# A graph network's last layer: the weight product moved from before the edge sum to behind it

## The chip, the cores and the metric

The kernel runs on one core of a Trainium2 chip. A core has a matrix engine (TensorE, PE in the profile, with its weight loads as PEld), a vector engine (VectorE, DVE), a scalar engine (ScalarE, ACT), GpSimd (POOL), which here issues the indirect loads, and SyncE (SP), which issues the plain ones; sixteen DMA engines move the data. The metric is device time of one execution in microseconds (us), less is better. Times in the profile count from the start of its span.

## The reference

A graph of N = 4096 nodes with D = 512 features and E = 65536 edges, sorted by destination, goes through four layers, each with a layer norm and a ReLU ahead of it and a residual sum behind it. Layers 0 (attention), 1 and 2 (messages) are not changed. The last layer is:

```python
# ahead of it: h = maximum(layernorm(x), 0)
row = concatenate([src, arange(n)]); col = concatenate([dst, arange(n)])   # each node is its own neighbour too
deg = segment_sum(ones, row, n)
dis = rsqrt(deg)
norm = dis[row] * dis[col]
z   = h @ W.T + b                                    # 512 x 512
out = segment_sum(norm[:, None] * z[row], col, n)
x   = x + relu(out)
```

The factor dis[col] is the same for all edges of one destination and can stand outside the sum. So can the product with W, since it is linear: the sum of dis[row] * (h[row] @ W.T + b) is (the sum of dis[row] * h[row]) @ W.T plus (the sum of dis[row]) * b.

## The kernel before, in words

All is float32. The 4096 nodes are 32 blocks of 128 rows, the 65536 edges 512 tiles of 128, and four tiles are a group (U = 4, 128 groups). A float32 array `acc` holds 32 x 530 numbers per partition in SBUF: one row of sums per node, of which the first 512 columns are used by the layers here. Under `manual_schedule` each engine runs its instructions in the order in which the code issues them, and SP's queue is ordered likewise.

**Layer 2's end** (`layer2_ends`, from 4578 to 5104 us of the profile) works through 16 pairs of blocks as a software pipeline: pass p of its loop does the first step of pair p, the second of pair p-1, and so on.

- Pair p: `load_h` (L1203) loads two blocks of h into `h_sb` (three buffers; `h2_sb` in the code). `turned` (L1251) transposes them on PE, 8 transposes of 128x128 into PSUM tile `tr`, and ACT copies them to `h_t` (L1253). The same for two blocks of `acc` (`a_t`). POOL then adds b4 to `h_sb` in place.
- Pair p-1: PE multiplies both by w3 into `u_ps` (L1276), ACT puts it into `zu` with the bias and computes the activation.
- Pair p-2: PE multiplies by w4 into `o_ps` (L408, `product`), DVE adds the two blocks of `h_sb` to it (L1294) and with that frees the buffer. A norm, the residual, the store of x3 (L1308), and the norm of layer 3 follow on DVE; the normed rows stay in `h3`.
- Pair p-4, layer 3's beginning: `turned` transposes `h3` with a ReLU on the way out, PE multiplies by layer 3's weights `wl_sb` into `o_ps` (L408), ACT multiplies by dis into `acc` (L1322), DVE adds dis * b (L1323), and SP stores the pair to the DRAM table `ztab` (L1324), rows of 512 floats.

**Layer 3's edge loop** (`sum_edges`, 5104 to 5869 us). For each tile POOL issues one indirect DMA (L419) that gathers 128 rows of `ztab`, by the edges' sources, into `g` (six buffers of four tiles), four groups ahead. One group ahead, ACT makes the one-hot matrices of the edges' places in their window of 128 destinations (L863 four times, L864 once per group; `oh`, three buffers). PE multiplies each one-hot with its gathered rows (L887), adding up a group of four tiles in one PSUM bank `sum_ps` (four banks). A group's window spans at most two blocks, so `add_window` adds the bank twice to `acc`, each with a mask of rows and the block's number read from a register (L431, on DVE). `acc` begins with the node's own row, from layer 2's end.

Inside this loop, after every second tile, `follow` is called. `Ending` closes a block b once the tiles are past a fixed place, `END_AT + END_STEP * b` = 230 + 10 b: ACT computes relu(dis * acc) into `t_end` (L1352), DVE adds x3's block, loaded ahead by SP into `x_end` (L1339), and SP stores it to the output (L1359). That these places are late enough for the data is checked on the device by `too_late`; data for which they are not would go through a general path behind it, which the inputs here do not take.

The same `sum_edges` serves layer 1 (1204 to 1996 us). There a class `Between` does the next layer's begin inside the loop, block by block: transposes, a copy by ACT to `ht_mid` (L980) and two products into `pq_ps` (L985).

Of the kernel before, what the change touches and what calls it, by code (L numbers as in the profile page):

```python
# [10 lines left out]
F32 = mybir.dt.float32  # L11
BF16 = mybir.dt.bfloat16
# [22 lines left out]
def kernel(  # L35
# [34 lines left out]
    PAIR = 2  # L70
    NW = NG // PAIR

    END_AT, END_STEP = 230, 10
    assert N == 4096 and E == 65536 and D == 512 and W == 512
    DA = D + H + 2
    HW = DA // 2
# [182 lines left out]
    def by_destination(pool, ppool):  # L259

        ends = pool.tile([P, 2, W], I32, name="ends_d")
        for j, of in enumerate((src, dst)):
            nc.sync.dma_start(ends[:, j, :], of.rearrange("(p c) -> p c", p=P))
        yield
        three = pool.tile([P, 3, W], F32, name="three_d")
        for j in range(2):
            nc.vector.tensor_copy(three[:, j, :], ends[:, j, :])
            yield
        loc_i = pool.tile([P, W], I32, name="loc_i")
        nc.vector.tensor_scalar(loc_i, ends[:, 1, :], P - 1, None, op0=OP.bitwise_and)  # L270
# [35 lines left out]
        for r in range(2):  # L306
            at = -(-(END_AT + END_STEP * r) // U)
            rows.append((first[:1, at::2 * END_STEP // U], P * (r + 1), 2 * P))
        too_late(pool, wide, rows)
        nc.vector.tensor_copy(odd[:, 1:2], wide)  # L310
        yield
# [542 lines left out]
    nc.vector.tensor_scalar(s_loc, s_loc, -1.0, None, op0=OP.mult)  # L854


    def sum_edges(table, idx, loc, bi, half, per, beside=None, follow=None):

        def made_one_hots(pool, minus, t0):

            oh = pool.tile([P, U, P], F32, name="oh")
            for j in range(U):
                nc.scalar.activation(oh[:, j, :], row_i, AF.Abs, bias=minus[:, t0 + j:t0 + j + 1])  # L863
            nc.scalar.activation(oh, oh, AF.Relu, scale=-1.0, bias=1.0)  # L864
            return oh

        with tc.tile_pool(name="edge", bufs=3) as ep, tc.tile_pool(name="edge_ps", bufs=4, space=PSUM) as eps, \
                tc.tile_pool(name="beside", bufs=1) as bp, \
# [3 lines left out]
            side = Side(*(beside(bp, bps) if beside else ()))  # L872
            for i in range(-4, NG):
                if i + 4 < NG:
                    g = got[i + 4] = ep.tile([P, U, D], F32, name="g", bufs=6)
                    for j in range(U):
                        t = (i + 4) * U + j
                        gather(g[:, j, :], table, idx[:, t:t + 1])
                if 0 <= i + 1 < NG:
                    ohs[i + 1] = made_one_hots(ep, loc, (i + 1) * U)  # L880
                if i < 0:
                    continue
                g, oh = got.pop(i), ohs.pop(i)
                if i % per == 0:
                    ps = eps.tile([P, D], F32, name="sum_ps")
                for j in range(U):
                    nc.tensor.matmul(ps, oh[:, j, :], g[:, j, :], start=i % per == 0 and j == 0,  # L887
                                     stop=i % per == per - 1 and j == U - 1)
# [299 lines left out]

        messages(begun)

    ztab = dram.tile([N, D], F32, name="ztab")
    x3 = dram.tile([N, D], F32, name="x3")
    def layer2_ends():
        with ExitStack() as end:
# [62 lines left out]
            end.enter_context(tc.manual_schedule(engines=ENGINES))  # L1257
            groups = NB // R
            h_t, a_t, u, xs, h3 = {}, {}, {}, {}, {}
            for p in range(groups + 4):  # L1260
                now = lambda k: 0 <= k < groups
                if now(p):
                    if p not in h:
# [33 lines left out]
                if now(p - 2):  # L1297
# [13 lines left out]
                    h3[p - 2] = lp.tile([P, R, D], F32, name="h3", bufs=3)  # L1311
                    for j in range(R):
                        norm.rows(j, h3[p - 2][:, j, :], xt[:, j, :])
                if now(p - 4):
                    b0 = (p - 4) * R
                    h3_t = turned("h3_t", h3.pop(p - 4), AF.Relu)
                    for j in range(R):
                        o_ps = lps.tile([P, D], F32, name="o_ps")
                        product(o_ps, h3_t[:, :, j * P:(j + 1) * P], wl_sb)
                        y = acc[:, b0 + j, :D]  # L1320
                        d = dis[:, b0 + j:b0 + j + 1]
                        nc.scalar.activation(y, o_ps, AF.Copy, scale=d)  # L1322
                        nc.vector.scalar_tensor_tensor(y, bl_bc, d, y, op0=OP.mult, op1=OP.add)  # L1323
                    nc.sync.dma_start(blocks_of(ztab, b0, R), acc[:, b0:b0 + R, :D])  # L1324

    layer2_ends()

    class Ending:


        def __init__(self, pool, ahead):
            self.pool, self.ahead, self.next, self.xs, self.ready = pool, ahead, 0, {}, []
# [16 lines left out]
        def begin(self):  # L1349
            b, self.next = self.next, self.next + 1  # L1350
            t = self.pool.tile([P, D], F32, name="t_end", bufs=4)
            nc.scalar.activation(t, acc[:, b, :D], AF.Relu, scale=dis[:, b:b + 1])  # L1352
            self.ready.append((b, t))

        def finish(self):
            for b, t in self.ready:
                xt = self.xs.pop(b)
                nc.vector.tensor_add(xt, xt, t)
                nc.sync.dma_start(out[b * P:(b + 1) * P, :], xt)  # L1359
                self.load(b + self.ahead)  # L1360
            self.ready = []

        def the_rest(self):
            self.finish()
            while self.next < NB:
                self.begin()
                self.finish()

    nc.vector.tensor_scalar(d_loc, d_loc, -1.0, None, op0=OP.mult)
    with tc.tile_pool(name="l3_end", bufs=1) as lp:  # L1370
        ending = Ending(lp, 6)
        sum_edges(ztab, d_src, d_loc, d_bi, d_half, 1, follow=ending.follow)
        ending.the_rest()

    @with_exitstack
    def in_general(ctx):
# [23 lines left out]
        def sums(table, k_from, k_to):  # L1400
            with tc.tile_pool(name="sums", bufs=1) as pool, tc.tile_pool(name="sums_ps", bufs=1, space=PSUM) as ppool:
                with tc.For_i(0, W, 1) as t:
                    rows = pool.tile([P, D], F32, name="rows_g")
                    gather(rows, table, number_of(pool, k_from, t))
                    over_blocks(pool, ppool, k_to, t, rows, 1)

        nc.sync.dma_start(by, stab.rearrange("k p w -> p k w"))
        for j in range(2):
# [111 lines left out]
                over_blocks(pool, ppool, 1, t, m, 1)  # L1520

        layer2_ends()
        sums(ztab, 0, 1)
        with tc.tile_pool(name="l3_late", bufs=1) as lp:
            Ending(lp, 6).the_rest()

    other = const.tile([1, 1], F32, name="other")
    nc.vector.reduce_max(other, odd, axis=AX.X)
# [39 lines left out]
```

## Time and profile before

| | us |
|---|---|
| median of nine runs | 5847.4 |
| lowest and highest of them | 5838.24, 5867.2 |
| the profiled execution | 5870.75 |
| its span in the profile | 5868.9 |
| PE, DVE, ACT, POOL busy | 5173.5, 3529.3, 3372.3, 2903.2 |
| layer 3's edge loop: matmuls L887, busy | 516.1 |
| its gathers L419, busy | 486.6 |

The profiled execution is one run, 23 us above the median, so differences are worked out in it and then put on the median. A row of the profile's groups reads: line, engine, operation, the tile written and the tiles read, how often; then busy time, mean ns of one, and the idle time of the engine just before them with what ended most of it. In a timeline a row begins with its start and its length, and the bracket at its end is the idle time before it and what released it. An f32 matmul of the program appears as two records, each a pass with its own weight load. "remote" and "issue" stand where the profile names no other engine.

### The profile page before, as it was taken

How to read it: one execution, taken by the hardware profiler on the slowest of the kernel's cores; microseconds unless marked ns; L12 is line 12 of the kernel's file. 1: busy time of each engine (PE TensorE's matmuls, PEld its weight loads, DVE VectorE, ACT ScalarE, POOL GpSimd, SP SyncE). 2: the span in 40 equal slices, each digit the busy share in tenths (PEclk: the TensorE clock that was granted, in tenths of full speed). 3: DMA queues.
4: the chain of work that ended last, by engine and by line, in shares of the span. 5: the costliest groups of instructions: out<-in, count | busy, mean ns of one | idle time of the engine just before them, and what ended most of it. 6: DMA issues, size and time to landing. Idle time of an engine off the chain costs nothing.

```text
span 5868.9 us, 56747 instructions
## 1 busy us (share of the span) xinstructions
PE 5173.5 (88%) x17274; PEld 2844.0 (48%) x17274; DVE 3529.3 (60%) x5843; ACT 3372.3 (57%) x5157; POOL 2903.2 (49%) x2604
## 2 busy tenths in 40 slices
PE   7678888869989799999999999999999899866676
PEld 4456666634434355555555555555555666422222
DVE  8566666623233377777777777777777456422223
ACT  1245555524334378888888888888888433333333
POOL 0255555456666465555555555555553111266665
PEclk9789899989999899999999999999999999988888
DMA  3356565467777565555555555555553212266676
GB/s 108 107 171 180 173 184 176 146 189 234 230 232 233 160 134 116 113 116 113 116 113 115 115 114 115 113 115 113 115 113 69 86 65 72 95 183 181 208 223 185
DMA packets 345928, 842.24 MB, mean 144 GB/s; under 512 B 61072, under 2 KB 77456, under 8 KB 345616
## 3 DMA queue, kind: packets, MB, share of 16 engines
q0 software_dynamic: 237568, 673.35, 47.0%
q1 hardware_dynamic: 108048, 165.19, 8.2%
q8 instruction: 140, 2.29, 0.2%
q14 instruction: 172, 1.41, 0.1%
HBM read 753.14 MB, written 85.20 MB: 143 GB/s over the span
## 4 chain that ended last, share of the span: by engine, by line
PE 68%; another core or an unknown queue 6%; ACT 3%; issue 3%; DVE 2%; DMA 1%; DVEq 1%; POOL 0%; SPq 0%; ACTq 0%; POOLq 0%
PE m_ps L408 30%; PE sum_ps L887 10%; PE small_ps L1084 4%; PE small_ps L1111 4%; PE o_ps L408 4%; PE tr_ps L1091 4%; PE u_ps L1276 4%; PE pq_ps L985 3%; PE sum_ps L696 2%; ACT oh L863 1%; DVE acc L431 1%; PE tr_ps L1074 1%; PE tr L1251 1%; ACT oh L864 1%
## 5 line engine op out<-in xcount | busy, mean ns | idle before, releaser
L408 PE MATMUL m_ps<-w_sb,h_t 128*128 128x512 f32 x4096 | 1820.8, 592 | 0.5 <-ACT h_t L1093 0.5
L887 PE MATMUL sum_ps<-g,oh 128*128 128x512 f32 x2048 | 1010.6, 636 | 257.6 <-ACT oh L864 103.2
L408 PEld LDWEIGHTS m_ps<-w_sb,h_t 128*128 128x128 f32 x4096 | 757.6, 190 | 809.3 <-issue 797.6
L419 POOL DMA_INDIRECT pg<-ptab,d_src x512 | 498.3, 973 | 993.5 <-ACT h_t L1093 817.0
L1067 POOL DMA_INDIRECT pg<-qtab,d_dst x512 | 871.4, 1702 | 158.2 <-issue 154.4
L419 POOL DMA_INDIRECT rows<-htab,s_dst x512 | 484.1, 945 | 654.4 <-issue 368.2
L887 PEld LDWEIGHTS sum_ps<-g,oh 128*128 128x128 f32 x2048 | 412.5, 205 | 802.2 <-issue 577.6
L696 PE MATMUL sum_ps<-rows,oh 128*128 128x261 f32 x2048 | 555.4, 423 | 198.2 <-DVE rows L690 123.8
L419 POOL DMA_INDIRECT g<-ytab,s_dst x512 | 485.3, 948 | 333.3 <-issue 132.8
L419 POOL DMA_INDIRECT g<-ztab,d_src x512 | 486.6, 950 | 329.6 <-issue 137.7
L696 PEld LDWEIGHTS sum_ps<-rows,oh 128*128 128x128 f32 x2048 | 412.1, 209 | 298.5 <-DVE rows L690 134.0
L1093 ACT COPY h_t<-tr_ps 128x512 f32<-128x512 f32 x512 | 275.2, 589 | 429.3 <-PE tr_ps L1091 429.2
L431 DVE SCALAR_TENSOR_TENSOR acc<-sum_ps,d_half,acc 128x512 f32 x256 | 192.3, 751 | 546.7 <-remote 275.5
L431 DVE SCALAR_TENSOR_TENSOR acc<-sum_ps,s_half,acc 128x522 f32 (+1 forms) x256 | 193.3, 755 | 406.5 <-PE sum_ps L887 257.6
L1143 DVE TENSOR_TENSOR pg<-pg,small_ps 128x512 f32<-128x512 f32 x512 | 318.3, 682 | 189.7 <-PE small_ps L1084 153.1
L1111 PE MATMUL small_ps<-parts,oh 128*128 128x512 f32 x1024 | 311.1, 446 | 13.4 <-DVE oh L414 13.4
L985 PE MATMUL pq_ps<-w_sb,ht_mid 128*128 128x512 f32 x512 | 270.5, 615 | 58.7 <-ACT ht_mid L980 54.4
L1105 DVE TENSOR_TENSOR parts<-z,parts 128x1024 fp32r<-128x1024 f32 x256 | 313.6, 1225 | 8.9
L863 ACT ACTIVATE oh<-row_i,d_loc 128x128 f32<-128x128 f32 x512 | 162.3, 387 | 269.7 <-remote 182.2
L1091 PEld LDWEIGHTS tr_ps<-ident,pg 128*128 128x128 f32 x2048 | 240.2, 141 | 146.2 <-issue 146.2
L1180 DVE TENSOR_TENSOR pg<-pg,qg 128x1024 f32<-128x1024 f32 x256 | 301.3, 1218 | 0.7 <-ACT qg L1177 0.7
L431 DVE SCALAR_TENSOR_TENSOR acc<-small_ps,d_half,acc 128x512 f32 x256 | 192.4, 751 | 161.4 <-issue 135.2
(281 smaller groups left out, 7959.3 us busy)
## 6 DMA issues: line engine op xcount, KB each, us to landing
eg<-in_edge_attr_dram SPq DMA_DIRECT2D x128, 128.0 KB
xt<-in_x_dram SPq DMA_DIRECT2D x8, 1024.0 KB
htab<-acc SPq DMA_DIRECT2D x32, 256.0 KB
x_row<-in_x_dram SPq DMA_DIRECT2D x32, 256.0 KB
rows<-htab,s_dst POOLq DMA_INDIRECT x512
x<-x_row SPq DMA_DIRECT2D x32, 256.0 KB
ytab<-acc SPq DMA_DIRECT2D x32, 256.0 KB
x_mid<-x SPq DMA_DIRECT2D x32, 256.0 KB
```

What stands on the lines that cost most here:

```text
L408: nc.tensor.matmul(ps, h_t[:, k, :], w_sb[:, k0 + k, :], start=start and k == 0, stop=stop and k == KC - 1)
L419: nc.gpsimd.indirect_dma_start(out=dst_ap, out_offset=None, in_=table, in_offset=bass.IndirectOffsetOnAxis(ap=idx, axis=0))
L431: nc.vector.scalar_tensor_tensor(at, ps, half[:, k, i:i + 1], at, op0=OP.mult, op1=OP.add)
L696: nc.tensor.matmul(ps[:, c, :HW], oh[:, j + k, :], rows[:, j + k, c * HW:(c + 1) * HW], start=j + k == 0, stop=j + k == GT - 1)
L887: nc.tensor.matmul(ps, oh[:, j, :], g[:, j, :], start=i % per == 0 and j == 0, stop=i % per == per - 1 and j == U - 1)
L985: nc.tensor.matmul(ps, h_t[:, k, :], self.w1_sb[:, k0 + k, :], start=k == 0, stop=k == KC - 1)
L1067: nc.gpsimd.indirect_dma_start(out=pg[:, j, :], out_offset=None, in_=qtab, in_offset=bass.IndirectOffsetOnAxis(ap=d_dst[:, t:t + 1], axis= ...
L1091: nc.tensor.transpose(h_ps[:, k, :], h[:, j, k * P:(k + 1) * P], ident)
L1105: nc.vector.tensor_sub(parts[:, 1], m, parts[:, 0].bitcast(F32))
L1111: nc.tensor.matmul(ps, oh[:, j, :], parts[j // 2][:, k, j % 2, :], start=j == 0 and k == 0, stop=j == U - 1 and k == 1)
L1143: nc.vector.tensor_add(nxt[:, j], nxt[:, j], ps)
L1180: nc.vector.tensor_mul(h[i][:, half], h[i][:, half], qg[:, half])
```

## The change

The transposes of `h3`, the product with `wl_sb` and its bias are taken out of layer 2's end. There ACT now writes relu(h3) * dis straight to `acc`, one pass of the pipeline earlier (pair p-3), and SP stores it to `ztab`. The table's rows get two more floats, which hold three bf16 numbers (and a fourth, not used) whose sum is dis, written once ahead of the pairs; column D of `acc` begins with dis, and the next two with zero.

In the edge loop a gather brings 514 floats. ACT makes a second one-hot in bf16 (`oh_short`), PE multiplies it with the three bf16 numbers into `tail_ps` ahead of the group's main matmuls, and DVE adds that to three more columns of `acc`, by `add_window` as for the rows.

`Ending` gets seven steps, one per call of `follow`: four transposes of acc's block into `turn_end`; ACT's copy to `ht_end`; two steps of two matmuls with `wl_sb` into `o_end`; the sum of the three columns times b, added to it, on DVE; ReLU and dis on ACT; the residual and the store. Its places are 150 + 20 b for the first eight blocks and 230 + 10 b as before for the others. `turn_end` and `o_end` have one PSUM bank each, the loads of x3 run four blocks ahead instead of six, and `wl_sb` and `bl_bc` are loaded at the start of `Ending`. The places' check and the general path are changed accordingly.

```diff
-    END_AT, END_STEP = 230, 10
+    ENDS = (0, 150, 20, 8), (8, 230, 10, NB)
+    def end_of(b):
+        return next(at + step * b for first, at, step, last in ENDS if b < last)
...
+    def tail_at(b):
+        return acc[:, ds(b, 1), D:D + 3].rearrange("p b d -> p (b d)")
...
             for j in range(U):
                 nc.scalar.activation(oh[:, j, :], row_i, AF.Abs, bias=minus[:, t0 + j:t0 + j + 1])
+            short = None
+            if tail:
+                short = pool.tile([P, U, P], BF16, name="oh_short")
+                nc.scalar.activation(short, oh, AF.Relu, scale=-1.0, bias=1.0)
             nc.scalar.activation(oh, oh, AF.Relu, scale=-1.0, bias=1.0)
...
-                    g = got[i + 4] = ep.tile([P, U, D], F32, name="g", bufs=6)
+                    g = got[i + 4] = ep.tile([P, U, D + tail], F32, name="g", bufs=6)
...
+                if tail:
+                    tail_ps = bps.tile([P, 3], F32, name="tail_ps", bufs=2)
+                    for j in range(U):
+                        nc.tensor.matmul(tail_ps, short[:, j, :], g[:, j, D:].bitcast(BF16)[:, :3],
+                                         start=j == 0, stop=j == U - 1)
                 for j in range(U):
-                    nc.tensor.matmul(ps, oh[:, j, :], g[:, j, :], start=i % per == 0 and j == 0,
+                    nc.tensor.matmul(ps, oh[:, j, :], g[:, j, :D], start=i % per == 0 and j == 0,
                                      stop=i % per == per - 1 and j == U - 1)
                     if j == U - 1 and i % per == per - 1:
+                        if tail:
+                            add_window(i, bi, half, tail_at, tail_ps)
                         add_window(i // per, bi, half, row_at, ps)
...
-    ztab = dram.tile([N, D], F32, name="ztab")
+    ztab = dram.tile([N, D + 2], F32, name="ztab")
...
-            wl_sb = load_w(wp, "wl_sb", w_l3t)
-            bl_bc = row_bc(wp, "bl_bc", b_l3)
+            three = wp.tile([P, NB, 4], BF16, name="dis_parts")
+            rest = wp.tile([P, NB], F32, name="dis_rest")
+            nc.vector.tensor_copy(rest, dis)
+            for k in range(3):
+                nc.vector.tensor_copy(three[:, :, k], rest)
+                nc.vector.tensor_sub(rest, rest, three[:, :, k])
+            nc.vector.tensor_copy(three[:, :, 3], rest)
+            nc.sync.dma_start(ztab[:, D:].rearrange("(b p) c -> p b c", p=P), three.bitcast(F32))
+            nc.vector.tensor_copy(acc[:, :, D], dis)
+            nc.vector.memset(acc[:, :, D + 1:D + 3], 0.0)
...
-            for p in range(groups + 4):
+            for p in range(groups + 3):
...
-                if now(p - 4):
-                    b0 = (p - 4) * R
-                    h3_t = turned("h3_t", h3.pop(p - 4), AF.Relu)
+                if now(p - 3):
+                    b0 = (p - 3) * R
+                    hh = h3.pop(p - 3)
                     for j in range(R):
-                        o_ps = lps.tile([P, D], F32, name="o_ps")
-                        product(o_ps, h3_t[:, :, j * P:(j + 1) * P], wl_sb)
-                        y = acc[:, b0 + j, :D]
-                        d = dis[:, b0 + j:b0 + j + 1]
-                        nc.scalar.activation(y, o_ps, AF.Copy, scale=d)
-                        nc.vector.scalar_tensor_tensor(y, bl_bc, d, y, op0=OP.mult, op1=OP.add)
-                    nc.sync.dma_start(blocks_of(ztab, b0, R), acc[:, b0:b0 + R, :D])
+                        nc.scalar.activation(acc[:, b0 + j, :D], hh[:, j, :], AF.Relu,
+                                             scale=dis[:, b0 + j:b0 + j + 1])
+                    nc.sync.dma_start(ztab[b0 * P:(b0 + R) * P, :D].rearrange("(b p) d -> p b d", p=P),
+                                      acc[:, b0:b0 + R, :D])
...
+        def block(self, b):
+            pool = self.pool
+            ps = self.ppool.tile([P, KC, P], F32, name="turn_end", bufs=1)
+            for k in range(KC):
+                nc.tensor.transpose(ps[:, k, :], acc[:, b, k * P:(k + 1) * P], ident)
+            yield
+            h_t = pool.tile([P, KC, P], F32, name="ht_end", bufs=2)
+            nc.scalar.copy(h_t, ps)
+            yield
+            ps = self.ppool.tile([P, D], F32, name="o_end", bufs=1)
+            for k in range(KC):
+                nc.tensor.matmul(ps, h_t[:, k, :], self.wl_sb[:, k, :], start=k == 0, stop=k == KC - 1)
+                if k % 2:
+                    yield
+            s = pool.tile([P, 1], F32, name="s_end", bufs=2)
+            nc.vector.reduce_sum(s, acc[:, b, D:D + 3], axis=AX.X)
+            t = pool.tile([P, D], F32, name="t_end", bufs=2)
+            nc.vector.scalar_tensor_tensor(t, self.bl_bc, s, ps, op0=OP.mult, op1=OP.add)
+            yield
+            nc.scalar.activation(t, t, AF.Relu, scale=dis[:, b:b + 1])
+            yield
+            xt = self.xs.pop(b)
+            nc.vector.tensor_add(xt, xt, t)
+            nc.sync.dma_start(out[b * P:(b + 1) * P, :], xt)
+            self.load(b + self.ahead)
...
         def follow(self, tiles):
 
-            if tiles % 4:
-                return
-            self.finish()
-            while self.next < NB and tiles >= END_AT + END_STEP * self.next:
-                self.begin()
+            if self.next < NB and not tiles % U and tiles >= end_of(self.next):
+                self.going.append(self.block(self.next))
+                self.next += 1
+            self.step()
```

More of the change, by code (lines that the diff above doesn't have):

```diff
@@ L305, in by_destination @@
         rows = []
-        for r in range(2):
-            at = -(-(END_AT + END_STEP * r) // U)
-            rows.append((first[:1, at::2 * END_STEP // U], P * (r + 1), 2 * P))
+        for b0, _, step, b1 in ENDS:
+            by = 1 if step % U == 0 else 2
+            for r in range(by):
+                at = -(-end_of(b0 + r) // U)
+                last = min(NG, at + (b1 - b0 - r - 1) // by * (by * step // U) + 1)
+                rows.append((first[:1, at:last:by * step // U], P * (b0 + r + 1), by * P))
         too_late(pool, wide, rows)
@@ L854, with sum_edges @@
     nc.vector.tensor_scalar(s_loc, s_loc, -1.0, None, op0=OP.mult)
-    def sum_edges(table, idx, loc, bi, half, per, beside=None, follow=None):
+    def sum_edges(table, idx, loc, bi, half, per, beside=None, follow=None, tail=0):
         def made_one_hots(pool, minus, t0):
@@ L1339, in load @@
                 nc.sync.dma_start(self.xs[b], x3[b * P:(b + 1) * P, :])
-        def follow(self, tiles):
-            if tiles % 4:
-                return
-            self.finish()
-            while self.next < NB and tiles >= END_AT + END_STEP * self.next:
-                self.begin()
[L1349 to L1361, printed above, removed]
-        def the_rest(self):
[L1364 to L1367, printed above, removed]
+        def block(self, b):
[23 more added lines that the diff above has]
+            self.load(b + self.ahead)
@@ new lines, in step @@
+        def step(self):
+            for w in list(self.going):
+                if next(w, StopIteration) is StopIteration:
+                    self.going.remove(w)
+        def follow(self, tiles):
+            if self.next < NB and not tiles % U and tiles >= end_of(self.next):
+                self.going.append(self.block(self.next))
+                self.next += 1
+            self.step()
+        def the_rest(self):
+            while self.next < NB or self.going:
+                if self.next < NB:
+                    self.going.append(self.block(self.next))
+                    self.next += 1
+                self.step()
+                self.step()
@@ L1369 @@
     nc.vector.tensor_scalar(d_loc, d_loc, -1.0, None, op0=OP.mult)
-    with tc.tile_pool(name="l3_end", bufs=1) as lp:
-        ending = Ending(lp, 6)
-        sum_edges(ztab, d_src, d_loc, d_bi, d_half, 1, follow=ending.follow)
+    with tc.tile_pool(name="l3_end", bufs=1) as lp, tc.tile_pool(name="l3_end_ps", bufs=1, space=PSUM) as lps, \
+            tc.manual_schedule(engines=ENGINES):
+        ending = Ending(lp, lps, 4)
+        sum_edges(ztab, d_src, d_loc, d_bi, d_half, 1, follow=ending.follow, tail=2)
@@ L1398, in over_blocks, with sums @@
                     nc.vector.tensor_add(at, at, ps)
-        def sums(table, k_from, k_to):
+        def sums(table, k_from, k_to, tail=0):
             with tc.tile_pool(name="sums", bufs=1) as pool, tc.tile_pool(name="sums_ps", bufs=1, space=PSUM) as ppool:
                 with tc.For_i(0, W, 1) as t:
-                    rows = pool.tile([P, D], F32, name="rows_g")
+                    rows = pool.tile([P, D + tail], F32, name="rows_g")
                     gather(rows, table, number_of(pool, k_from, t))
-                    over_blocks(pool, ppool, k_to, t, rows, 1)
+                    if tail:
+                        wide = pool.tile([P, DA], F32, name="wide_g")
+                        nc.vector.memset(wide[:, D:], 0.0)
+                        nc.vector.tensor_copy(wide[:, :D], rows[:, :D])
+                        nc.vector.tensor_copy(wide[:, D:D + 3], rows[:, D:].bitcast(BF16)[:, :3])
+                        over_blocks(pool, ppool, k_to, t, wide, 2)
+                    else:
+                        over_blocks(pool, ppool, k_to, t, rows, 1)
         nc.sync.dma_start(by, stab.rearrange("k p w -> p k w"))
@@ L1522, in in_general @@
         layer2_ends()
-        sums(ztab, 0, 1)
-        with tc.tile_pool(name="l3_late", bufs=1) as lp:
-            Ending(lp, 6).the_rest()
+        sums(ztab, 0, 1, 2)
+        with tc.tile_pool(name="l3_late", bufs=1) as lp, tc.tile_pool(name="l3_late_ps", bufs=1, space=PSUM) as lps:
+            Ending(lp, lps, 4).the_rest()
     other = const.tile([1, 1], F32, name="other")
```

10 lines of the change are left out of this document (6 added, 4 removed).

## The prediction

> **What bounds the kernel now.** First the page, by slices and groups: which engine fills which part of the span. Then the busy times of three stretches, for the clock and for which engine leads. Then the timeline at the two places that the change touches.
>
> ```profile
> PE   7678888869989799999999999999999899866676
> POOL 0255555456666465555555555555553111266665
> PEclk9789899989999899999999999999999999988888
> ...
> L419 POOL DMA_INDIRECT g<-ztab,d_src x512 | 486.6, 950 | 329.6 <-issue 137.7
> ...
> L985 PE MATMUL pq_ps<-w_sb,ht_mid 128*128 128x512 f32 x512 | 270.5, 615 | 58.7 <-ACT ht_mid L980 54.4
> ```
>
> The last five slices (146.7 us each) are layer 3's edge loop: PE 6 to 7 tenths, POOL as much, a lower clock. The slices before them (layer 2's end) have PE at 8 to 9 and hardly any POOL.
>
> ```profile
> core 0: us, PE busy (x) PEld busy (x) DVE busy (x) ACT busy (x) POOL busy (x), PEclk, DMA share, GB/s
> 4800.00:4900.00 100.00, 96.66 (x377) 65.28 (x376) 56.75 (x136) 40.10 (x47) 13.99 (x6) 1.00 0.19 64
> 5200.00:5300.00 100.00, 66.38 (x140) 28.27 (x139) 26.20 (x35) 32.75 (x88) 66.33 (x71) 0.86 0.64 185
> 5700.00:5800.00 100.00, 72.94 (x150) 30.25 (x149) 29.72 (x41) 37.74 (x97) 67.70 (x72) 0.87 0.74 223
> ```
>
> So layer 2's end (4578 to 5104 us) is bound by PE at full clock, and the loop (5104 to 5869) is not. A gather takes 0.95 us and the next follows 0.30 later: 512 x 1.25 = 640 us of the loop's 765. The change takes PE work out of the first stage and puts it into the second. Its worth is what the first can give up less what the second can't hide.
>
> **Layer 2's end: what goes.** A steady pair of blocks takes 31.55 us. The removed part (8 transposes 0.87, the wait for ACT's copy 1.11, 16 passes of 0.43) is 9.02 us by the timeline, 4871.11 to 4880.13. But that work covers a load. h_sb (h2_sb in the code) has three buffers, so the load for pair p+1 is issued only after DVE's second add (L1294) of pair p-2, which is right behind the w4 product; then the removed products run. Where there are none yet (pairs 3 and 4) the profile shows what is left:
>
> ```profile
> 4624.04 0.69 DVE L1294 TENSOR_TENSOR acc<-h_sb,o_ps 128x512 f32<-128x512 f32 x1 [2.69 <-PE o_ps L408]
> 4624.81 0.36 SPq L1203 DMA_DIRECT2D h_sb<-h  x1
> 4628.73 1.94 PE L1251 MATMUL tr<-ident,h_sb 128*128 128x128 f32 x8 [4.72 <-DMA h_sb<-h]
> ...
> 4654.44 0.36 SPq L1203 DMA_DIRECT2D h_sb<-h  x1
> ...
> 4657.97 1.94 PE L1251 MATMUL tr<-ident,h_sb 128*128 128x128 f32 x8 [4.28 <-DMA h_sb<-h]
> ```
>
> PE waits 4.72 and 4.28 us for h_sb, then runs at half clock (eight transposes 1.94 instead of 1.04) for 3.4 to 6.8 us. From 4628.73 to 4657.97 is 29.24 us per pair. I take 31.55 - 9.02 + 4.5 + 1.6 (half clock) = 28.6; ends 22.5 (load hidden) and 29.24. Pair 15 is then turned at 4657.97 + 11 x 28.6 = 4972.6, 24.1 us of its iteration follow, and the last u product (13.82) ends at 5010.5, where before has 5051.8: 41 earlier. Behind it before needs 52.3 us to its last ztab store (two more rounds of products); after needs the w4 product 6.9, DVE's chains of the last two pairs (14.7 and 13.6) and two Relus of about 0.7: 36.5. Together -41 - 16, taken as **-56** (with all pairs at 29.24: -50; with the load hidden: -115). The bf16 parts of dis are ten small DVE operations and one 4096-row store ahead of pair 0; the nearest row, the store of 4096 x 32 B at L560, was 2.6 us of packets. The wl loads go from the same place: nothing, -3 to +3.
>
> **Layer 3's loop, tiles up to 310.** Added per group: one ACT Relu (0.63 as L864), four bf16 passes (eight of L656 took 0.42: 0.21), two DVE adds with a register address (0.82 apart as L431's), and eight blocks in all. PE, DVE and ACT are idle for a third to two thirds of this stretch, so the pace of 1.44 us per tile hides them, except that the Relu stands in ACT's restart, once per 20 tiles: 15 x 0.63 = **+9**. Rows of 2056 instead of 2048 B: htab's 2080 B gathers took 0.94 us of all 16 DMA engines against 0.905, and DMA is busy 0.64 to 0.74, so hidden; without that cover 512 x 0.03 = 15. Bounds -45 (pace 1.29, near the 1.25 of POOL, if the denser PE ends the pauses shown next) to +20 (blocks prolong eight pauses).
>
> ```profile
> 5822.94 10.57 PE L887 MATMUL sum_ps<-g,oh 128*128 128x512 f32 x24 [0.81 <-ACT oh L864]
> ...
> 5830.54 0.95 POOL L419 DMA_INDIRECT g<-ztab,d_src  x1 [0.30 <-issue]
> ...
> 5834.82 3.28 DVE L431 SCALAR_TENSOR_TENSOR acc<-sum_ps,d_half,acc 128x512 f32 x4 [10.41 <-PE sum_ps L887]
> 5835.06 0.94 POOL L419 DMA_INDIRECT g<-ztab,d_src  x1 [3.58 <-remote]
> ...
> 5840.74 2.08 PE L887 MATMUL sum_ps<-g,oh 128*128 128x512 f32 x2 [7.24 <-issue]
> ```
>
> This is the loop's cycle, every 28.6 us: PE does three groups in a row (24 passes), yet DVE and POOL see the first of them done only when PE has stopped and 1.3 us have gone. PE's completions come late, POOL runs out of g buffers for 3.6 us, and 20 gathers take 25 + 3.6.
>
> **Tiles 310 to 512: a block every 10 tiles.** A pass of 128x512 takes 0.43 and an f32 product two of them (1024 records for 512 tiles). PE's own work per block is 10 x 0.857 + 2.5 x 0.21 (tails) + 4 x 0.108 (transposes) + 8 x 0.43 (product) = 12.96 us, under the 14.4 that ten tiles take now. But the transposes stand in PE's queue right behind a group's last matmul and read acc, which DVE's row adds of that same group write at register addresses: PE must wait for DVE, which waits for PE. Queued behind them are all later matmuls, and so g buffers and gathers. The price: two adds 1.57 and some 0.4 of handover, 1.95, if the completion comes at once (5858.09, after the last matmul, does); about 1.6 more with the late completions above: 3.55. Then the product waits for ACT's copy of the turned block; layer 1's loop has that wait (L985) at 54.4 us in 32 blocks, 1.7 each. Here half a group of matmuls lies more between: I take half, 0.85. Sum 17.4 per block, 20.2 x 17.4 = 351 us against 291 now: **+60**. Ends: the pace stays 14.4 (0), and 22 (+153), where DVE has the adds of two or three groups (3.3 each with the tails) to catch up on before the transposes may run.
>
> **Drain and start.** Before ends its last add 5 us after the last matmul. After: block 28's turning and blocks 29 to 31 come behind it, one turn_end and one o_end bank, so about 5.0 each (0.43 + 0.59 + 3.43 and handovers), then STT, Relu, add (0.75, 0.72, 0.68) and waits: 26.5, **+22** (ends +14, +30). Start: 1.25 MB of wl and bl stand on SP ahead of x_end and share the DMA with the first gathers: **+3** (0 to 8).
>
> **Sum:** -56 + 9 + 60 + 22 + 3 = +38 us. The profiled execution took 5870.75 (span 5868.9) and would take 5909; the median of the nine runs is 5847.4, so 5885.
>
> A rule that speaks against this sum: the Trainium skill, "TensorE: Matmul & The Clock Gate", section "Why this matters for your kernels", says that PE idle for more than about 3 us falls back to half clock. The trace agrees on its sides: 4.28 us of idle was followed by half clock, the waits of 2.0 to 2.85 us in layer 1's loop left the clock at 0.98. By the rule each block's 3.55 us would also cost 1.7 to 3.4 us, an estimate of +34 to +69 on top; my sum takes none, since 3.55 lies between those two rows.
>
> **Rivals.** (1) *The loop hides the blocks*, faster: PE has 1.44 us of room per block under the gathers' 14.4, and if the late completions end because POOL then pauses at other times, the turning costs no more than that. It decides at a wait of 1.45 us per block. Then -56 + 9 + 0 + 22 + 3 = -22, 5825; with a better early pace down to 5790. For it: the last groups' completions were prompt. Against: two adds alone are 1.57. (2) *Near tie*: all waits of a block cost 2.5 us, what layer 1's loop shows (16 tiles 23.5 us, PE work 21.0): 15.5 per block, +22 instead of +60, so 5847. (3) *The load is hidden after all*: -115 instead of -56, 5826. Against: both uncovered pairs waited. (4) *DVE catches up*: 20 to 22 per block, +113 to +153, so 5938 to 5978. For it: the quoted cycle, with two groups' adds in one go and PE idle 7.24 us.
>
> **Chances.** Forecast 0.42, (1) 0.22, (2) 0.11, (3) 0.07, (4) 0.18. Faster by over 0.2% (11.7 us, about what can be told from no change): (1) and (3), 0.29; within: (2) and a little of the forecast's low end, 0.13; slower: 0.58. The range cuts the ends of (1) and the upper half of (4): 5800 to 5950; the forecast's own is 5860 to 5915.
>
> **What would show it.** The steps in the changed profile: PE waiting 4 to 5 us for h_sb in every pair, pairs 28 to 29 us apart; the first gather at 5050 instead of 5108; tiles 310 to 512 in 335 to 370 us, with turn_end's transposes waiting for DVE's acc and o_end's matmuls for ht_end; 20 to 30 us from the last sum matmul to the end. Pairs of 23 us, or blocks at 14.4 us, would make it wrong towards faster; PE idle of over 7 us before each block's transposes towards slower.

## The result and the profile after

The changed kernel takes 5944.42 us (median of ten runs) against 5849.5 for the kernel before: a ratio of 1.0158, interval 1.0141 to 1.0175. It is 1.6% slower where 0.64% slower was forecast; 95 us stand against a sum of 38. The profiled execution has a span of 5964.4 us. Its slices:

```profile
PE   7678788869999799999999999999999888576788
...
POOL 0255555356666465555555555555551111665553
PEclk9789989989999899999999999999999889788899
```

Layer 2's end (slices 32 to 34) now has a clock of 8 to 9 tenths where it had 9; over the stage the mean is 0.89 instead of 0.99. The loop's share of POOL falls from 6 tenths to 5 behind its first third.

Later runs fell on chips of two kinds, which this comparison didn't show: on one kind the kernel before takes 5789 to 5865 us, on the other 5420 to 5424. The result above is of the first, slow kind. Each chip was used in one session only, so whether the chip itself makes the kind is not shown; "slow" and "quick" stand for what was measured there. Stages are compared within a kind. All stages are read from the traces, one execution for each column, in us:

| | slow: before | after | quick: before | after |
|---|---|---|---|---|
| layer 2's end, first transposes to first gather | 526.1 | 491.5 | 526.4 | 494.7 |
| first gather to first sum matmul | 7.2 | 10.2 | 7.4 | 10.4 |
| tiles 0 to 150 | 219.9 | 233.9 | 183.7 | 183.8 |
| tiles 150 to 310 | 231.6 | 273.6 | 201.1 | 211.3 |
| tiles 310 to 512 | 290.3 | 331.8 | 254.1 | 324.8 |
| last sum matmul to the end | 11.4 | 33.0 | 12.4 | 32.9 |
| span | 5868.9 | 5964.4 | 5421.9 | 5493.5 |

On the slow chip the stages give +87.5; the other 8 us lie ahead of layer 2's end, in code that is the same. On slow chips a stage with gathers differs by a few us from run to run: tiles 0 to 150 take 231 to 239 us in the traces of the changed kernel and of the experiments that leave these tiles alone.

The timeline of the changed kernel at the head of a steady pair in layer 2's end:

```profile
4813.51 0.36 SPq L1222 DMA_DIRECT2D h_sb<-h  x1
...
4817.97 1.94 PE L1278 MATMUL tr<-ident,h_sb 128*128 128x128 f32 x8 [5.21 <-DMA h_sb<-h]
...
4819.70 1.91 PE L1278 MATMUL tr<-ident,acc 128*128 128x128 f32 x8
...
4821.41 3.12 PE L1303 MATMUL u_ps<-h_t,w_sb 128*128 128x256 f32 x8
...
4824.37 1.89 PE L1303 MATMUL u_ps<-a_t,w_sb 128*128 128x256 f32 x8
```

PE waits 5.21 us for the load, and from 4817.97 to about 4823.8 it runs at half clock: both sets of transposes take 1.9 instead of 1.04, the first eight passes 3.12 instead of 1.89. The pair takes 30.7 us.

The same kernel in the loop, where a block comes every 20 tiles:

```profile
5359.65 3.68 PE L904 MATMUL sum_ps<-g,oh 128*128 128x512 f32 x8
...
5365.56 0.75 DVE L436 SCALAR_TENSOR_TENSOR acc<-sum_ps,d_half,acc 128x512 f32 x1 [2.80 <-issue]
...
5369.81 0.22 DVE L436 SCALAR_TENSOR_TENSOR acc<-tail_ps,d_half,acc 128x3 f32 x1 [3.50 <-issue]
5370.09 0.94 POOL L424 DMA_INDIRECT g<-ztab,d_src  x1 [2.59 <-remote]
...
5371.61 1.57 DVE L436 SCALAR_TENSOR_TENSOR acc<-sum_ps,d_half,acc 128x512 f32 x2 [0.67 <-DVE acc L436]
...
5373.32 1.09 PE L1371 MATMUL turn_end<-ident,acc 128*128 128x128 f32 x4 [9.99 <-DVE acc L436]
...
5374.35 4.91 PE L904 MATMUL sum_ps<-g,oh 128*128 128x512 f32 x8
```

The group's matmuls end at 5363.3, DVE adds them at 5371.61, and only then can PE turn the block: 9.99 us idle, and half clock after it (8 passes 4.91 instead of 3.68). DVE is not adding all this time: it is busy for 2.7 of the 9.99 us, and ahead of the two operations marked "issue" it sat idle for 2.80 and 3.50 us without waiting for anything that the profile shows. In the nine waits of 9.87 to 10.42 us, one for each block from tile 150 to 312, DVE is busy 2.0 to 3.5 us.

Ahead of the first sum matmul:

```profile
5088.84 0.16 PE L901 MATMUL tail_ps<-g,oh_short 128*128 128x3 bf16 x1 [31.36 <-DMA g<-ztab,d_src]
...
5092.10 0.16 PE L901 MATMUL tail_ps<-g,oh_short 128*128 128x3 bf16 x1 [0.97 <-DMA g<-ztab,d_src]
```

The four tail matmuls of a group stand ahead of its sum matmuls, so the first sum matmul now waits for the fourth gather, 3.3 us after the first. And behind the last sum matmul:

```profile
5934.62 0.63 PE L1371 MATMUL turn_end<-ident,acc 128*128 128x128 f32 x4 [2.63 <-DVE acc L436]
...
5942.65 1.96 PE L1378 MATMUL o_end<-wl_sb,ht_end 128*128 128x512 f32 x4 [0.93 <-DVE s_end L1382]
...
5947.70 1.95 PE L1378 MATMUL o_end<-wl_sb,ht_end 128*128 128x512 f32 x4 [0.93 <-DVE t_end L1384]
...
5952.74 3.67 PE L1378 MATMUL o_end<-wl_sb,ht_end 128*128 128x512 f32 x8 [0.93 <-DVE t_end L1384]
...
5958.05 0.69 DVE L1389 TENSOR_TENSOR x_end<-x_end,t_end 128x512 f32<-128x512 f32 x1 [0.85 <-ACT t_end L1386]
```

The products start 5.05 us apart, each waiting for the one o_end bank.

### The profile page after: what moved, and what is told of

Same layout as the page of the kernel before. It is cut to its first block, busy times and chain, and to the rows that moved or that the text cites. A ratio compares the mean times of both kernels' runs of the same rounds, so it can differ in the third digit from the quotient of the medians.

```text
span 5964.4 us, 59542 instructions
## 1 busy us (share of the span) xinstructions
PE 5221.1 (88%) x17786; PEld 2885.9 (48%) x17786; DVE 3596.4 (60%) x6144; ACT 3452.2 (58%) x5301; POOL 2915.9 (49%) x2605
## 5 line engine op out<-in xcount | busy, mean ns | idle before, releaser
L1110 PE MATMUL tr_ps<-ident,pg 128*128 128x128 f32 x2048 | 266.3, 273 | 10.5 <-DVE pg L1199 10.5
```

The source lines that it names most:

```text
L1110: nc.tensor.transpose(h_ps[:, k, :], h[:, j, k * P:(k + 1) * P], ident)
```

## The experiments

Theory 1: in layer 2's end the products that were taken out had covered a load. Theory 2: in the loop PE stands at the transposes until DVE has caught up, because completions come late; the rival is a plain handover. All edits are made to the changed kernel where nothing else is said.

**A fourth buffer for h_sb** (slow chip).

```diff
-                t = lp.tile([P, R, D], F32, name="h2_sb", bufs=3)
+                t = lp.tile([P, R, D], F32, name="h2_sb", bufs=4)
```

> The changed kernel with four h_sb buffers instead of three in layer 2's end, so that a pair's load can go out one pair earlier. Theory 1 (the removed products had covered that load): PE's wait of 5.2 us for h_sb goes in every steady pair, and with it the half clock behind it; pairs of 22.5 to 23.5 us instead of 30.7, the first gather some 85 us earlier, and the whole time 75 to 90 us below the changed kernel, about level with the kernel before. Rival (the pair is bound by something else that has grown, such as DVE's norm operations of 2.8 us beside POOL's adds): pairs stay at 28 us or more and less than 30 us are won.

The whole takes 5856.86 us, 0.9982 of the kernel before (0.9962 to 1.0001). Layer 2's end takes 387.1 us instead of 491.5, the loop the same 840.0. Its timeline at the head of a pair:

```profile
4796.93 1.04 PE L1278 MATMUL tr<-ident,h_sb 128*128 128x128 f32 x8
...
4797.80 1.04 PE L1278 MATMUL tr<-ident,acc 128*128 128x128 f32 x8
4797.85 0.36 SPq L1222 DMA_DIRECT2D h_sb<-h  x1
...
4798.68 1.89 PE L1303 MATMUL u_ps<-h_t,w_sb 128*128 128x256 f32 x8
```

No bracket: PE doesn't wait, the load that goes out here is the next pair's, 21.5 us ahead of its transposes, and pairs take 22.4 us. Theory 1 is shown: one buffer is worth 104 us in this stage, more than the 85 that were expected, and with it the change comes level.

**No blocks in the loop, and no tails** (slow chip, two kernels).

```diff
-            if self.next < NB and not tiles % U and tiles >= end_of(self.next):
+            if False:
```

> The changed kernel, but no block is closed inside the loop: all 32 are turned, multiplied and stored behind it. The tails stay. Theory 2 (in the loop it is the turning's wait for DVE that costs): from the first to the last sum matmul 742 to 755 us as before's 742, where the changed kernel takes 839; behind the loop 140 to 170 us. Rival (the tails, with their extra ACT, PE and DVE work in every group, slow the loop): over 770 us from first to last matmul.

From the first to the last sum matmul 757.4 us, where before takes 741.9 and the changed kernel 839.3; behind the loop 177.1. Both are a little above what was expected.

```diff
-                short = pool.tile([P, U, P], BF16, name="oh_short")
-                nc.scalar.activation(short, oh, AF.Relu, scale=-1.0, bias=1.0)
+                pass
...
-                        if tail:
-                            add_window(i, bi, half, tail_at, tail_ps)
```

> The changed kernel without the tails' work: no bf16 one-hot, no tail matmuls, no tail adds; the bias is then weighted by the node's own factor alone. Blocks stay where they are. Theory 2 with a share of the tails in DVE's backlog (up to three groups to add before a turning may run, 1.6 us of tail adds in each): loop 20 to 40 us shorter than the changed kernel's 839. Rival A (tails are hidden): within 10 us of 839. Rival B (tails are the cost): down to 760 or less.

786.3 us, 53 less than the changed kernel where 20 to 40 were expected. So the tails alone cost 15 us, the blocks alone 44, both 97, by single runs: more together than apart. Why is not shown: the tails add work to ACT and PE as well as to DVE.

**The blocks ten tiles apart from tile 230** (slow chip).

```diff
-    ENDS = (0, 150, 20, 8), (8, 230, 10, NB)
+    ENDS = (0, 230, 10, NB),
```

> The changed kernel with all blocks ten tiles apart from tile 230 on (the places of the kernel before), instead of eight blocks 20 tiles apart from tile 150. Theory 2: a block is dear (5.3 us) where PE has run several groups in a row and DVE has them all to add, and cheap (2.05 us) at one per ten tiles; so tiles 150 to 230 return to 120 us, tiles 230 to 310 take 131, and the whole is 20 to 30 us below the changed kernel. Rival (a fixed price per block, wherever it stands): no change within 8 us.

5925.97 us (1.0101 of before, 1.0057 to 1.0145). Tiles 150 to 230 take 115.7 us, 230 to 310 141.3: 257.0 instead of 273.6, and the loop 811.9. A block isn't of one price: where blocks are dense, each costs less. In the trace the first block's transposes (tile 232) wait 7.44 us, those of the next seven 1.75 to 3.00, where blocks 20 tiles apart wait some 10.

**The turning moved away from the add** (on quick chips). In the one kernel a block begins two tiles later; in the other, DVE copies the finished sums to a buffer of their own, which PE turns eight tiles later.

```diff
-            if self.next < NB and not tiles % U and tiles >= end_of(self.next):
+            if self.next < NB and tiles % U == 2 and tiles - 2 >= end_of(self.next):
```

> The changed kernel with each block begun two tiles later, in the middle of a group, so that two tiles of matmuls stand between a group's last matmul and the transposes that wait for DVE's adds of it. Theory 2 (DVE gets the groups' completions late and in a bunch, and PE stands at the transposes until it has added them all): the waits of about 10 us ahead of the transposes in tiles 150 to 310 become at most 2 us shorter, the loop 10 to 30 us shorter than 839. Rival (a plain handover: two adds and a signal): the waits disappear and the loop falls by 60 us or more.

```diff
+            kept = pool.tile([P, D], F32, name="kept", bufs=3)
+            nc.vector.tensor_copy(kept, acc[:, b, :D])
+            yield
+            yield
+            yield
+            yield
...
-                nc.tensor.transpose(ps[:, k, :], acc[:, b, k * P:(k + 1) * P], ident)
+                nc.tensor.transpose(ps[:, k, :], kept[:, k * P:(k + 1) * P], ident)
```

> The changed kernel with a copy on DVE between: a finished block's sums are copied to a buffer of their own in DVE's order, and PE turns that buffer eight tiles later, so that PE no longer waits for the adds of the group that it has just finished. Theory 2: PE's waits ahead of the transposes go nearly all, tiles 150 to 310 take 230 to 250 us (273 in the changed kernel, 232 before), tiles 310 to 512 take 300 to 320 (332, 290); behind the loop 5 to 15 us more, since more blocks are open at its end. Rival (the product's 4 us of PE per block and its other handovers are the price): tiles 150 to 310 stay above 260.

Loops of 649.2 and 647.8 us, on a chip where the kernel before takes 5423; the transposes inside the loop don't wait at all. To compare, both kernels and the copy once more on a quick chip:

> The kernel before, unchanged, for a profile on the same chip as the next three, since the chips differ: on the chip of the runs without turning waits the kernel before takes 5423 us instead of 5850. If PE's late completions belong to the chip, this profile shows a loop of 640 to 670 us on a chip of 5420 and of 742 on a chip of 5850. Rival (the chips differ in all stages alike): 742 x 5423 / 5850 = 688 us, and layer 2's messages 7% shorter too.

> The changed kernel, unchanged, beside the kernel before on the same chip. Tiles 310 to 512 take 325 to 335 us on either kind of chip, since there PE's own stops at the turning set the pace (326 in the run with half rows on a chip of 5423, 332 in the first run on a chip of 5850). Tiles 150 to 310 take 205 to 215 where completions are prompt, 273 where they are late.

> The copy on DVE between (each block turned from a buffer of its own, eight tiles later), beside the two above. Theory 2: on a chip with prompt completions tiles 310 to 512 take 262 us, 13.0 per block, which is PE's own work of 12.96; on one with late completions 290 to 310, and 240 to 260 for tiles 150 to 310. Rival (the late completions hold the product as much as the turning): there no gain over the changed kernel.

The loops are 638.8 before, 719.8 after, 648.7 with the copy; the spans 5421.9, 5493.5 and 5412.3. So the kinds differ in the gather loops and not in layer 2's end. On a quick chip DVE follows at once: its first add of a group begins at the median 0.0 us after the end of its last matmul, by the traces, where the slow chip has 6.2 us and more than 4 in 58% of the groups (the kernel before on both). The changed kernel on the quick chip, two turnings of tiles 310 to 512:

```profile
5217.91 1.56 DVE L436 SCALAR_TENSOR_TENSOR acc<-sum_ps,d_half,acc 128x512 f32 x2 [4.07 <-PE sum_ps L904]
...
5219.61 0.63 PE L1371 MATMUL turn_end<-ident,acc 128*128 128x128 f32 x4 [1.75 <-DVE acc L436]
...
5235.82 1.58 DVE L436 SCALAR_TENSOR_TENSOR acc<-sum_ps,d_half,acc 128x512 f32 x2 [1.02 <-issue]
...
5237.54 1.09 PE L1371 MATMUL turn_end<-ident,acc 128*128 128x128 f32 x4 [3.00 <-DVE acc L436]
```

This is the plain handover: two adds and a signal, 1.75 us, or 3.00 where DVE has the block before's bias and the tails in its queue first; behind the 3.00 PE is at half clock (1.09 for 0.63). With the copy, PE goes through. Windows of busy time, of the changed kernel and then of the one with the copy:

```profile
core 0: us, PE busy (x) PEld busy (x) DVE busy (x) ACT busy (x) POOL busy (x), PEclk, DMA share, GB/s
5150.00:5400.00 250.00, 215.32 (x646) 96.89 (x644) 96.95 (x200) 110.47 (x255) 149.18 (x156) 0.95 0.69 195
```

```profile
5100.00:5350.00 250.00, 244.98 (x792) 112.88 (x791) 125.60 (x263) 138.31 (x324) 189.63 (x199) 1.00 0.82 247
```

PE is busy 98% at full clock instead of 86% at 0.95, and a block takes 261.8 / 20.2 = 13.0 us against 16.1: PE's own work was put at 12.96.

**The same two and half rows on a slow chip.**

> The copy on DVE between, alone on the changed kernel, for a chip with late completions (kernel before at 5850 us). Theory 2 in that case: the loop falls from 839 to between 760 and 800 us, since PE no longer stands at the transposes for 10 us; what is left over 742 are the tails (15 us, as without blocks) and the product. Rival (the late completions then hold PE at the product or at the one-hots instead): 815 or more. On a chip of 5422 it repeats 649.

> Each block begun two tiles later, in mid-group, for a chip with late completions. Theory 2: DVE's catching up is what PE waits for there, so two tiles of cover take away under 2 us of some 10: loop 800 to 835. Rival (plain handover): below 780. On a chip of 5422 it repeats 649, as the rival has it.

778.5 and 782.1 us, from 839, in single runs. Two tiles of cover win about as much as the copy. The expectation for the two tiles, 800 to 835, is missed towards the rival, whose bound of 780 is just missed too: also where DVE comes late, what costs is that PE stands exactly there, and two tiles of work ahead of the transposes give 57 of the 97 us back. The waits don't vanish on this kind: in tiles 150 to 310 the transposes wait 5.5 us in the mean, instead of 10.2. With the copy they don't wait in the loop, but in tiles 310 to 512 PE stands 27.8 us ahead of the products.

```diff
-    ztab = dram.tile([N, D + 2], F32, name="ztab")
+    ztab = dram.tile([N, D // 2 + 2], F32, name="ztab")
...
+                        into = ps.rearrange("p (r d) -> p r d", r=2)
+                        rows = g[:, j, :D // 2].unsqueeze(1).to_broadcast([P, 2, D // 2])
```

> The changed kernel with half of each gathered row left out: layer 3's table has 256 columns and the two tail numbers, and PE reads the half row twice, so its matmuls keep their size; all else is as it was, but the DMA bytes of the gathers are halved. Theory 3 (PE's completions reach the others late because the gathers' DMA traffic keeps them waiting; in the trace of before they arrive about 1 us after the last gather packet of each cycle): completions come within 2 us, PE's waits ahead of the transposes in tiles 150 to 310 fall from 10 to under 4 us, and the loop takes 700 to 770 us instead of 839. Rival (they are late for a cause in PE or in the order of the program): waits of 10 us stay and the loop stays above 810.

> Half of each gathered row left out and the half row read twice by PE, for a chip with late completions. Theory 3 (the gathers' traffic holds PE's completions back there): loop 720 to 760, as the 721 of a chip with prompt completions. Rival (the cause is not the bytes): 810 or more. On a chip of 5422 it repeats 721.

On the quick chip the loop with half rows takes 721.4 us (719.8 with whole ones), on the slow one 841.0 (839.3). The gathers move 66 MB instead of 131 in it, and the loop changes by less than 2 us; theory 3 falls.

**A short stop for POOL in each group** (slow kind; before takes 5788.9 there in a single run).

```diff
+                    if follow:
+                        nc.gpsimd.tensor_add(pause, pause, pause)
```

> The kernel before with a small POOL addition (128x160, about 0.75 us with what lies around it) behind every four gathers of layer 3's loop, so that POOL issues no more than four gathers in a row. Theory 4, for a chip with late completions: they are held while POOL issues gathers back to back and come through when it stops, so with a stop in each group they are prompt: DVE's lag behind PE falls under 2 us and the loop stays at 730 to 750 us, although POOL alone now needs 128 x 5.75 = 736. Rival (the stops change nothing of it): the pauses of 3.6 us every 20 gathers stay on top of 736, the loop takes 800 to 840. On a chip with prompt completions (kernel before at 5422) 736 to 745, which tells nothing of it.

> The same POOL addition in the changed kernel. Theory 4 on a chip with late completions: PE's waits of 10 us ahead of the transposes fall to 3 or 4, and the loop comes to 770 to 800 us, below the 839 without the addition. Rival: 850 or more. On a chip with prompt completions 760 to 790, where tiles 310 to 512 stay at 325.

737.7 and 828.7 us. The first lies in theory 4's bounds, but DVE's lag, on which it rests, stays: more than 4 us in 45% of the groups (58% without the stops, on another chip). The second misses both sides: the waits ahead of the transposes are 8.3 us in the mean, where theory 4 had 3 or 4, the lag is as frequent as without the stops (30% of the groups), and 828.7 lies between 770 to 800 and the rival's 850. Theory 4 is not borne out, but not ruled out either for the kernel before: that chip's loop without the stops was not profiled, and its layers 0 and 1, which the stops leave alone, take 67 us less than on the chip of the first profile.

**All together**: four buffers, blocks ten tiles apart, the copy.

> Four h_sb buffers, blocks ten tiles apart from tile 230, and the copy on DVE, together on the changed kernel. Theories 1 and 2 add up: 89 us by the buffer and 27 by the places as measured alone, 15 to 35 by the copy; 5795 to 5830 us, 0.5 to 1% below the kernel before. Rival (the gains in the loop are one gain twice): no faster than the buffer and the places alone, 5830 or more.

> Four h_sb buffers, blocks ten tiles apart from tile 230, and the copy on DVE. On a chip of 5423: 5317 again. On a chip of 5850: 5780 to 5830, 0.3 to 1.2% below the kernel before; the rival (the loop's gains are lost to late completions there) gives 5835 to 5860.

> Four h_sb buffers, blocks ten tiles apart from tile 230 and the copy on DVE, for a chip with late completions: loop 760 to 790, the whole 5790 to 5830 us beside 5850 to 5865 of the kernel before. Rival: loop above 805 and the whole 5835 or more. On a chip of 5422 it repeats 5317.

On a quick chip 5316.62 us, 0.9804 of the kernel before (0.9787 to 0.982), and 5317.38 on another, 0.9808 (0.9792 to 0.9824); on a slow one 5780.89, 0.9871 (0.9843 to 0.9899). This version beats both kernels on both kinds.

## Why the prediction was right and wrong

- **The sign and the shape** were right: the loop loses more than layer 2's end wins. Of the waits that were named, those for h_sb, for DVE's acc and for the one o_end bank are in the profile; o_end's matmuls waiting for ht_end are not. By stages, against the sum: layer 2's end 21 us too favourable, tiles up to 310 47 too favourable, tiles 310 to 512 19 too dear, start and drain as put; the other 8 us lie in code that is the same.
- **Layer 2's end, -56**: the mechanism (uncovered load, half clock behind it) is shown by the fourth buffer. The size is off: 34.6 us won. The term that failed is "31.55 - 9.02 + 4.5 + 1.6 (half clock) = 28.6": the wait is 5.21 and half clock lasts 5.8 us, which costs 2.9, so 30.7; over the eleven pairs that is 22 us, all that is missing. The model, pairs 3 and 4 of before, had no store of ztab half a microsecond behind the load. On the quick chip the load takes 4.2 to 4.6 us to land in these pairs, and 3.7 to 3.8 in the two of before; that the store does this was not tried. The tail of the stage was right: from the last u product to the first gather 40.3 us instead of 56.4, 16 less as worked out.
- **Tiles up to 310, +9**: this step failed. It let the loop's slack hide everything but a Relu; measured are +56 on the slow chip, 16 of them also with the blocks out (467.8 us against 451.5), the rest with the eight blocks, whose transposes hold PE for some 10 us each. The bound of +20 was too near as well. Rival (4) had named waits of that length, but behind tile 310 and for another reason, DVE adding two or three groups: in these waits DVE is busy 2.0 to 3.5 us and idle for the rest. On a quick chip the step's number is met, 10.3, but by luck: tiles 0 to 150, which have the Relu too, cost 0.1, and the other 10.2 stand where the blocks are turned, with waits of 1.66 to 3.48 us.
- **Tiles 310 to 512, +60**: 41.5 on the slow chip, 70.7 on the quick one. The price of a block was put at 17.4; it is 16.4 and 16.1. PE's work of 12.96 agrees with the 13.0 of the copy; the wait of 3.55 is 2.7 and 2.3 in the mean (1.75 to 3.25 but for one of 10.42), half clock adds 0.9 and 0.8 at most; the 0.85 for the copy by ACT isn't there. The 14.4 us that ten tiles took before belong to the slow chips; on a quick one they take 12.6, so the same block costs 3.5 there instead of 2.0.
- **Drain +22** was right: 21.6. Products 5.05 us apart were put at 5.0. **Start +3** was right by luck: it is 3.0, but not for the loads of wl and bl, to which it was put. Without the tails, where these loads are the same, the first sum matmul follows the first gather after 7.2 us as before; the 3 us are the tail matmuls' wait for the fourth gather.
- **The clock rule** that was weighed is the Trainium skill's, "TensorE: Matmul & The Clock Gate", section "Why this matters for your kernels": idle over some 3 us brings half clock. In tiles 310 to 512 of the changed kernel's two traces none of 20 waits of 1.75 us was followed by half clock, and 11 of 12 waits of 2.98 to 3.01 were, though not always at once. But 3 us is no firm limit: in layer 1's loop of before six of 21 waits of 2.0 to 2.2 us were followed by 3.4 us at half clock, which the mean of 0.98 hides. The sum left the rule out, saying 3.55 lay between two rows, and was in the wrong there; the price is smaller than the 34 to 69 us that were weighed, 15 to 19 at most, since only 31 to 38 us of these tiles passed at half clock.
- **Still open**: why DVE follows PE's matmuls late on the slow chips. The prediction, and theory 2 with it, said that PE's completions come late. In the kernel before DVE mostly does wait for them, but in the changed kernel DVE's own sequencer is slow too. Ahead of each add it reads the block's number into a register; the shortest step of that takes 0.02 us each time on the quick chip, and some 0.7 us in 30 of 509 cases on the slow one, though it waits for nothing. The gathers' bytes are not the cause; POOL's unbroken issuing is not settled. What differs in those chips was not tried.

## What to carry to other kernels

Before work is taken out of an engine's queue, look what it covered: here 9 us of products hid a 5 us load, and one more buffer was worth 104 us, more than the whole change cost. Where PE must wait for DVE's result of PE's own last group, put two tiles of other work between; that alone gave back 57 to 71 us. And look for the same change's price on more than one chip: the stage that cost 42 us on one kind cost 10 on the other.

## What had not been expected of the hardware

The chips fell into two kinds. Between layer 1's last gather and layer 2's end both take the same (2615 and 2618 us), but layer 3's loop, with one gather and one matmul per tile, takes 742 us on one and 639 on the other, where it runs at POOL's own 1.25 us per gather; from the first gather to the last, layer 0 takes 902 and 656, layer 1 763 and 668. On the slow kind DVE's first add in layer 3 begins 6.2 us after a group's matmuls at the median, and over 14 in an eighth of the groups.

In layer 2's end of the changed kernel DVE's operations of 0.75 us take 2.85 when they run beside one of POOL's additions:

```profile
4818.59 0.75 DVE L1331 SCALAR_TENSOR_TENSOR acc<-acc,st,gamma_bc 128x512 f32<-128x512 f32 x1
...
4820.05 2.37 POOL L1294 TENSOR_TENSOR h_sb<-h_sb,b_bc 128x1024 f32<-128x1024 f32 x1 [25.60 <-PE tr L1278]
4820.11 2.85 DVE L1331 SCALAR_TENSOR_TENSOR acc<-acc,st,gamma_bc 128x512 f32<-128x512 f32 x1
```

DVE's operation ends 0.5 us after POOL's. It lies off the path here.
